# One more batch by seven products, masks loaded into the weights' tiles, and W1's operands split over two stages

## The chip, the cores and the metric

The kernel runs on one core of one Trainium2 chip. The metric is the device time of one launch in microseconds (us). The engines are named PE (matrix products), ACT (ScalarE), DVE (VectorE), POOL (GpSimd) and SP (SyncE). SP, ACT and POOL issue DMA transfers from their own instruction queues.

## The reference

```python
# x: (8, 256, 1024); mask: (8, 1024, 1024) of 0 or 1; W, b, W1, b1: one for all batches
# layer 0
y = x + x @ W.T + b + coeff[:, None, None] * (x @ (2 * mask - 1))
# layer 1: each batch picks one of 32 adapters of rank 16
h = y @ A[adapter]                      # (8, 256, 16)
out = y + y @ W1.T + b1 + 2.0 * (h @ Bm[adapter])
```

Everything is float32. The first layer has another weight matrix in each batch: `I + W.T + coeff * (2 * mask - 1)`. The second layer has one matrix, `I + W1`, for all.

## The kernel before, in words

**Groups.** The eight batches run in two groups of four. For each group comes a first layer, batch by batch, and then a second layer for the four batches together. The output tiles `y` of a group stay on the chip between the two.

**First layer, plain form.** A batch's weight matrix is made in eight pieces of 128x1024 (512 KB). Piece `k` is piece `k % 8` of batch `k // 8`. `load` has SP fetch the mask into an int32 tile `m` of `mpool` (3 tiles), four pieces ahead; it also fetches `x`, `W0` in batch 0, and W1's sixteen blocks `w1` spread over the pieces from 10 on. `build` has ACT turn the mask into `2c*m - c` in a weight tile `w` of `wpool` (3 tiles; L227), and DVE add `W0` (L230), two pieces ahead of the products. `first_batch` (L280) and `first_layer` (L255) multiply; ACT evicts with the bias (L267). Batches 0 to 3 run in this form.

**First layer, seven products.** The class `Seven` splits weights and tokens into 2x2 blocks and needs seven block products in place of eight (L388), at 128 columns each, with the operands `s1` to `s4` (sums of weights, L326) and `t1` to `t4` (sums of tokens, L342). PE's order is X `a11`, Y `a12`, X `s2`, Z `s1`, X `s3`, Z `s4`, X `a22`. X and Z are read in between (L403, L408). Batches 4 to 7 run in this form, with their weights in tiles of `wpool`, `tpool` and `qpool`.

**Second layer.** It takes the seven-product scheme twice, one inside the other: seven outer products `A11, A12, S1, S2, S4, S3, A22`, one call of `run` each, and in each of these seven inner ones with the left operands `a11, s1, s2, a12, s3, a22, s4` ("leaves", 256 KB each, L643). Forty-nine leaves are derived from W1: S1 to S4 are sums of quarters of W1 (`outer`, L539), and each outer operand has its inner sums (`inner`, L522 to L528). `combine_weights` makes them on DVE beside the first layer of group 0, three or four sums after each piece, and `keep` has POOL store each leaf in DRAM (L489). S3 alone is made later, beside runs 1 and 2. `load_leaves` has SP fetch the seven leaves of the next run into `lpool` (7 tiles), as the tiles come free. The right operands are sums of `y`: T1 to T4 (`outer_sum`, L634) and their inner sums `t1` to `t4` (L604 to L610).

Within a run, a bank X gathers four inner products in turn, and each value is read (L694 by ACT where nothing is to be added, L695 by DVE) before the next product adds to it. The next run's first product, `begin`, lies between `s3` and `a22`.

**Adapters.** `begin_adapters` and `load_adapters` clear `lb_pad` and `h_sb` on POOL and issue sixteen small DMAs there: four times `b1` and ones, and for each batch its `la` (64 KB) and rows of `lb_pad`. They hang on a value of `y` of batch 2, half 0. `down` (L675) multiplies `y` by `la` in run 0 of the second layer, after its first two products; `up` (L660) adds the adapters' result through ACT (L669).

**Order.** A scheduler places the instructions on each engine in program order by its own estimate of times, and `tc.issue_after` (in the kernel's words, `behind(...)`) keeps an instruction behind a named one. On the chip each queue runs in that fixed order. Tiles of a pool are given out as they come free.

Of the kernel before, what the change touches and what calls it, by code (L numbers as in the profile page):

```python
# [9 lines left out]
F32 = mybir.dt.float32  # L10
# [9 lines left out]
SEVEN = (4, 5, 6, 7)  # L20
# [4 lines left out]
def kernel(  # L25
# [50 lines left out]
    mpool = ctx.enter_context(tc.tile_pool(name="mask", bufs=3))  # L76
    wpool = ctx.enter_context(tc.tile_pool(name="weff", bufs=3))
# [59 lines left out]
    x_sb, m_sb, weff, raw, weff_at = {}, {}, {}, {}, {}  # L137
# [33 lines left out]
    def load(k: int):  # L171


        b, h, g = pieces[k]
        m_sb[k] = mpool.tile([P, 2, OH], I32, tag="m", name=f"m_{k}")
        pairs = [(m_sb[k], mask[b, g if b == 0 else h * NG + g])]
# [16 lines left out]
        else:  # L193
            for t, a in pairs:
                nc.sync.dma_start(t, a)
# [6 lines left out]
        for n, (q, r) in enumerate(W1_ORDER):  # L202
            if k == 0 and r % 2 == 0:
                two = pair(f"w1_{q}_{r // 2}")
                raw[q, r], raw[q, r + 1] = two[:, 0], two[:, 1]
            if k == 2 * NG + 2 + 3 * n // 4:
                nc.sync.dma_start(raw[q, r], w1T[q, r])

    def build(k: int):
# [8 lines left out]
        if b not in SEVEN or (h == 0 and g < 3):  # L218
            pool, tag = wpool, "w"
        elif g >= NG // 2:  # L220
            pool, tag = tpool, "T"
        else:
            pool, tag = qpool, "q"
        w = pool.tile([P, CG, OH], F32, tag=tag, name=f"w_{k}")
        m = m_sb.pop(k)
# [6 lines left out]
        weff[k] = w  # L232
# [8 lines left out]
    def first_layer(b: int, h: int, y, beside):  # L241
# [3 lines left out]
        for g in range(NG):  # L245
            k = (b * 2 + h) * NG + g
            if k + LOADS_AHEAD < n_pieces:
                load(k + LOADS_AHEAD)
# [22 lines left out]
    def first_batch(y, beside):  # L271

        ps = [bank(f"ps1_0_{i}") for i in range(NC // 2)]
        for c in range(NC):
            load(c + LOADS_AHEAD)
# [26 lines left out]
    H = T // 2  # L302

    class Seven:
# [3 lines left out]
        def __init__(self, b: int):  # L308
            self.b = b
            self.w, self.t = {}, {}  # L310
            self.ps = {}

        def block(self, i, j, a):
# [4 lines left out]
            if k + LOADS_AHEAD < n_pieces:  # L318
                with behind("leaves"):
                    load(k + LOADS_AHEAD)  # L320
# [3 lines left out]
        def weight_sum(self, n, op, x, y, a):  # L324
            s = self.w[n, a] = qpool.tile([P, CG, OH], F32, tag="q", name=f"{n}_{self.b}_{a}")
# [6 lines left out]
        def token_sum(self, n):  # L332
            t = self.t[n] = lpool.tile([P, TPH, H], F32, tag="l", name=f"{n}_{self.b}")
            for a in range(2):
# [7 lines left out]
                nc.vector.tensor_sub(o, x, y)  # L342
# [34 lines left out]
        def half(self, dest, left, right, a, first=False):  # L377
# [4 lines left out]
            for c in range(CG):  # L382
# [4 lines left out]
                for j in range(TPH):  # L387
                    nc.tensor.matmul(  # L388
# [18 lines left out]
        def add(self, i, v, ps):  # L407
            nc.vector.tensor_add(self.out(i, v), ps, self.out(i, v))  # L408

        def products(self):  # L410
# [9 lines left out]
            self.add(0, 0, ps["Y"])  # L420
# [7 lines left out]
            self.with_bias(1, 1, ps["Z"])  # L428
            for a in range(2):
                self.half("X", "s3", "t3", a)  # L430
                yield
            self.add(1, 1, ps["X"])
            for a in range(2):
# [15 lines left out]
    class Sevens:  # L449
# [7 lines left out]
        def begin(self, early: int):  # L457
            while self.made < early:
                next(self.operands, None)
# [31 lines left out]
    later = []  # L491

    def combine_weights():
# [17 lines left out]
        def inner(name, blocks, own, place=None):  # L511
            a11, a12, a21, a22 = (blocks[u, v] for u in range(2) for v in range(2))
            s = {}
            for n in ("s1", "s2", "s3", "s4"):
                if place is None:
                    s[n] = lpool.tile([P, CG, OQ], F32, tag="l", name=f"{name}_{n}")
                else:
                    if n in ("s1", "s3"):
                        two = pair(f"{name}_{n}")
                    s[n] = two[:, n in ("s2", "s4")]  # L520
# [9 lines left out]
                yield  # L530
            for n, t in (("a11", a11), ("a12", a12), ("a22", a22)):
                if n in own:
                    keep(name, n, t)

        def outer(name, op, x, y):
            tiles = [tpool.tile([P, 2, CG, OQ], F32, tag="T", name=f"{name}_{u}") for u in range(2)]
            out = {(u, v): tiles[u][:, v] for u in range(2) for v in range(2)}
# [3 lines left out]
            quads[name] = out  # L541

# [8 lines left out]
        yield from inner("A22", quads["A22"], ("a11", "a22"))  # L551
        yield from outer("S1", nc.vector.tensor_add, quads["A21"], quads["A22"])
        yield from inner("S1", quads["S1"], every)
        yield from outer("S2", nc.vector.tensor_sub, quads["S1"], quads["A11"])
        yield from inner("S2", quads["S2"], every)
# [432 lines left out]
```

## Time and profile before

| | us |
|---|---|
| median of 3 runs | 411.32 |
| lowest and highest | 409.96, 411.5 |
| the profiled execution, its own time | 410.92 |
| its span, from the first to the last instruction | 409.1 |
| PE busy | 403.8 |
| DVE busy | 300.7 |
| first layer of group 0: end of its products | 117.8 |
| second layer of group 0: end of its products | 211.4 |
| first layer of group 1: end of its products | 312.0 |

The profile is of one execution. Its page gives the busy time of each engine, then the span in 40 slices of 10.2 us with the busy share in tenths, the DMA queues, the chain of work that ended last, and the costliest groups of instructions. Timelines list instructions by start time, with the idle time before them and what ended it in brackets. A line such as L255 is a line of the kernel before.

### The profile page before, as it was taken

The page shows a single profiled execution, that of the slowest core. Times are in us where ns is not written, and L with a number is a line of the kernel's source. Part 1 is how long each engine was busy: PE and PEld are TensorE (multiplying, and loading weights), DVE is VectorE, ACT ScalarE, POOL GpSimd, SP SyncE. Part 2 cuts the span into 40 slices and gives each one's busy share as a digit, 9 for nine tenths or more (in the row PEclk, how much of TensorE's full clock was granted, in tenths as well). Part 3 has the DMA queues.
Part 4 walks back from the last instruction along what each step waited for, and adds up shares of the span by engine and source line. Part 5 has one row for each costly group of instructions (what it writes and reads, how often), then busy time and mean ns, then how long its engine had stood idle before and what let it go on. Part 6 is the DMA issues. An engine that isn't in the chain of part 4 may idle for free.

```text
span 409.1 us, 6555 instructions
## 1 busy us (share of the span) xinstructions
PE 403.8 (99%) x2458; PEld 358.2 (88%) x2458; DVE 300.7 (74%) x427; ACT 136.0 (33%) x213; POOL 38.6 (9%) x77
## 2 busy tenths in 40 slices
PE   8999999999999999999999999999999999999996
PEld 6888888888887888888899999999998788888885
DVE  2438598886647558994999999999936365886493
ACT  4434534543445201133115648174221420102200
POOL 0000042575201001000000000400000000000000
PEclk9999999999999999999999999999999999999999
DMA  8999799999987476767795758662122247554654
GB/s 274 405 402 387 274 371 414 412 393 331 414 331 256 134 234 199 220 218 201 241 367 162 263 184 302 202 215 96 26 74 66 75 145 230 173 154 162 213 154 154
DMA packets 41762, 97.44 MB, mean 238 GB/s; under 512 B 5508, under 2 KB 6276, under 8 KB 41732
## 3 DMA queue, kind: packets, MB, share of 16 engines
q1 hardware_dynamic: 32690, 76.17, 55.2%
q0 software_dynamic: 4288, 12.61, 8.1%
q10 hardware_dynamic: 4754, 8.26, 5.4%
q8 instruction: 19, 0.31, 0.3%
q14 instruction: 11, 0.09, 0.1%
HBM read 77.09 MB, written 19.92 MB: 237 GB/s over the span
## 4 chain that ended last, share of the span: by engine, by line
PE 91%; DMA 5%; ACT 2%; SPq 1%; DVE 0%; issue 0%; DVEq 0%; ACTq 0%
PE X L643 24%; PE ps L255 20%; PE X L388 12%; PE Z L643 12%; PE Z L388 6%; PE Y L643 6%; DMA m<-mask 5%; PE ps L280 4%; PE Y L388 3%; PE G L660 2%; PE psh L675 2%; ACT w L227 1%; ACT y L403 0%; SPq L186 0%; DVE w L230 0%
## 5 line engine op out<-in xcount | busy, mean ns | idle before, releaser
L227 ACT ACTIVATE w<-m,neg_c,two_c 128x1024 f32<-128x1024 int32 (+1 forms) x67 | 80.1, 1203 | 109.9 <-DMA m<-mask 40.7
L230 DVE TENSOR_TENSOR w<-w,w_sb 128x1024 f32<-128x1024 f32 (+1 forms) x67 | 77.4, 1172 | 36.9 <-ACT w L227 32.7
L255 PE MATMUL ps<-x,w 128*128 128x256 f32 x384 | 83.3, 379 | 0.0
L255 PEld LDWEIGHTS ps<-x,w 128*128 128x128 f32 x384 | 72.9, 190 | 10.2 <-DVE w L230 0.4
L778 DVE TENSOR_TENSOR c<-c,e 128x512 f32<-128x512 f32 x48 | 32.0, 683 | 3.9 <-ACT c L669 3.8
L388 PE MATMUL X<-t,s 128*128 128x128 f32 x256 | 30.0, 276 | 0.0
L388 PEld LDWEIGHTS X<-t,s 128*128 128x128 f32 x256 | 29.2, 192 | 0.2 <-ACT y L403 0.2
L280 PE MATMUL ps<-x,w 128*128 128x256 f32 x128 | 28.7, 385 | 0.2 <-DVE w L230 0.2
L669 ACT COPY c<-G 128x512 f32<-128x512 f32 x32 | 16.4, 600 | 36.4 <-PE G L660 33.1
L280 PEld LDWEIGHTS ps<-x,w 128*128 128x128 f32 x128 | 24.8, 194 | 4.2 <-DVE w L230 0.8
L695 DVE TENSOR_TENSOR c<-X,c 128x512 f32<-128x512 f32 (+1 forms) x26 | 16.7, 647 | 15.1 <-PE X L643 15.0
L403 ACT ACTIVATE y<-X,b_sb 128x128 f32<-128x128 f32 x48 | 13.6, 366 | 39.6 <-PE X L388 39.6
L694 ACT COPY e<-X 128x512 f32<-128x512 f32 x16 | 9.4, 588 | 48.0 <-PE X L643 41.7
L643 PE MATMUL X<-T_t,l_S_s 128*128 128x256 f32 x96 | 22.8, 380 | 0.0
L643 PEld LDWEIGHTS X<-T_t,l_S_s 128*128 128x128 f32 x96 | 18.2, 190 | 2.7 <-DVE e L695 0.3
L326 DVE TENSOR_TENSOR s<-w,w 128x1024 f32<-128x1024 f32 x16 | 19.2, 1215 | 0.0
L695 DVE TENSOR_TENSOR e<-X,e 128x512 f32<-128x512 f32 x16 | 10.9, 684 | 6.6 <-PE X L643 6.6
L643 PE MATMUL X<-b_t,l_A_s 128*128 128x256 f32 x64 | 15.5, 386 | 0.0
L388 PE MATMUL Z<-x,s 128*128 128x128 f32 x128 | 15.0, 276 | 0.0
L388 PE MATMUL Y<-x,w 128*128 128x128 f32 x128 | 14.9, 275 | 0.0
L388 PE MATMUL Z<-t,s 128*128 128x128 f32 x128 | 14.9, 275 | 0.0
L388 PE MATMUL X<-t,w 128*128 128x128 f32 x128 | 14.9, 275 | 0.0
(125 smaller groups left out, 622.4 us busy)
## 6 DMA issues: line engine op xcount, KB each, us to landing
m<-mask SPq DMA_DIRECT2D x61, 512.0 KB, 6.1
l_S_s<-leaf_S_s SPq DMA_DIRECT2D x32, 256.0 KB, 2.7
x<-xT SPq DMA_DIRECT2D x31, 256.0 KB, 7.8
outT<-c ACTq DMA_DIRECT2D x30, 256.0 KB, 3.5
l_A_s<-leaf_A_s SPq DMA_DIRECT2D x24, 256.0 KB, 2.7
l_S_a<-leaf_S_a SPq DMA_DIRECT2D x24, 256.0 KB, 2.7
w<-w1T SPq DMA_DIRECT2D x16, 256.0 KB, 6.4
leaf_S_s<-S_s POOLq DMA_DIRECT2D x16, 256.0 KB, 7.0
```

The lines of the kernel that those rows point to most:

```text
L227: nc.scalar.activation(w[:, i], m[:, i], AF.Identity, bias=neg_c[:, b : b + 1], scale=two_c[:, b : b + 1])
L230: weff_at[k] = nc.vector.tensor_add(w[:, i], w[:, i], w0_of(k)[:, i])
L255: nc.tensor.matmul(ps[j // 2][:, j % 2, :], lhsT=w[:, c, j * P : (j + 1) * P], rhs=x_sb[b, g][:, c, :],  start=first and j % 2 == 0, stop= ...
L280: nc.tensor.matmul(ps[ot // 2][:, ot % 2, :], lhsT=w[:, h, j * P : (j + 1) * P], rhs=x_sb[0, c // CG][:, c % CG, :], start=c == 0 and ot % ...
L326: anchors["weights"] = op(s, self.w[x, a], self.w[y, a])
L388: nc.tensor.matmul(ps[:, j, :], lhsT=w[:, c, j * P : (j + 1) * P], rhs=r, start=first and a == 0 and c == 0 and j == 0, stop=False, skip_g ...
L403: nc.scalar.activation(self.out(i, v)[:, j, :], ps[:, j, :], AF.Identity, bias=b0_sb[:, ot : ot + 1])
L643: nc.tensor.matmul(ps[:, j, :], lhsT=l[:, c, j * P : (j + 1) * P], rhs=r[:, c, :], start=first and c == 0 and j == 0, stop=False, skip_gro ...
L669: nc.scalar.copy(dest[b // 2][u, b % 2], ps[b])
L694: return nc.scalar.copy(out, ps)
L695: anchors["reads"] = nc.vector.tensor_add(out, ps, other)
L778: nc.vector.tensor_add(o, o, x)
```

## The change

Masks are loaded straight into the weights' tiles, which are seen as int32 until ACT has converted them in place; `mpool` is gone and `wpool` has six tiles. Batch 3 joins the seven-product form. Its weights lie in `tpool` and `wpool`, and its `s3` and `s4` overwrite `a11` and `a12`. W1's blocks are loaded two for each piece from piece 8 on. S2 and S4 are written over A11 and A12, and S1 lies in `qpool`. The inner sums of A22 and S2 are made during batch 3 (`mid`, `late`), those of S4 beside run 0, and S3, whose inputs POOL loads again, beside runs 1 and 2; S4 and S3 are made in place. The adapters are begun in `mid` of batch 3, on a value of its `y`. Masks 32 to 35 are loaded after run 1, and two more after run 5. Group 1's first weights are built beside run 5. The products of the second layer, `up` and `down` are also held in the written order by `behind`.

```diff
-SEVEN = (4, 5, 6, 7)
+SEVEN = (3, 4, 5, 6, 7)
...
-    mpool = ctx.enter_context(tc.tile_pool(name="mask", bufs=3))
-    wpool = ctx.enter_context(tc.tile_pool(name="weff", bufs=3))
+    wpool = ctx.enter_context(tc.tile_pool(name="weff", bufs=6))
...
-        m_sb[k] = mpool.tile([P, 2, OH], I32, tag="m", name=f"m_{k}")
-        pairs = [(m_sb[k], mask[b, g if b == 0 else h * NG + g])]
+        if b in SEVEN and k % (2 * NG) >= 6 and b >= GB:
+            pool, tag = qpool, "q"
+        elif b in SEVEN and b % 2 and k % (2 * NG) < 6:
+            pool, tag = tpool, "T"
+        else:
+            pool, tag = wpool, "w"
+        weff[k] = pool.tile([P, CG, OH], F32, tag=tag, name=f"w_{k}")
+        last = (k + 1) % (GB * 2 * NG) == 0
+        pairs = [(weff[k].bitcast(I32), mask[b, g if b == 0 else h * NG + g])]
...
-            if k == 2 * NG + 2 + 3 * n // 4:
+            if k == 2 * NG + n // 2:
                 nc.sync.dma_start(raw[q, r], w1T[q, r])
...
-        if b not in SEVEN or (h == 0 and g < 3):
-            pool, tag = wpool, "w"
-        elif g >= NG // 2:
-            pool, tag = tpool, "T"
-        else:
-            pool, tag = qpool, "q"
-        w = pool.tile([P, CG, OH], F32, tag=tag, name=f"w_{k}")
-        m = m_sb.pop(k)
+        w = weff[k]
+        m = w.bitcast(I32)
...
+    loaded = 0
+    def load_to(n: int):
+        nonlocal loaded
+        while loaded < min(n, n_pieces):
+            load(loaded)
+            loaded += 1
...
-            if k + LOADS_AHEAD < n_pieces:
-                load(k + LOADS_AHEAD)
+            n = k + LOADS_AHEAD + 1
+            load_to(min(n + max(0, n - (GB - 1) * 2 * NG), GB * 2 * NG))
...
+    SEVEN_AHEAD = 4
+    limit = GB * 2 * NG
...
-            if k + LOADS_AHEAD < n_pieces:
-                with behind("leaves"):
-                    load(k + LOADS_AHEAD)
+            with behind("leaves"):
+                load_to(min(k + SEVEN_AHEAD, max(k + 1, limit)))
             build(k)
...
-            s = self.w[n, a] = qpool.tile([P, CG, OH], F32, tag="q", name=f"{n}_{self.b}_{a}")
+            if self.b < GB and n in ("s3", "s4"):
+                s = self.w[x, a]
+            else:
+                s = qpool.tile([P, CG, OH], F32, tag="q", name=f"{n}_{self.b}_{a}")
+            self.w[n, a] = s
             anchors["weights"] = op(s, self.w[x, a], self.w[y, a])
...
-            self.add(0, 0, ps["Y"])
+            with behind("weights") if self.b < GB else nullcontext():
+                self.add(0, 0, ps["Y"])
...
             self.with_bias(1, 1, ps["Z"])
+            self.mid()
             for a in range(2):
...
             self.add(1, 1, ps["X"])
+            self.late()
             for a in range(2):
...
-        def inner(name, blocks, own, place=None):
+        def inner(name, blocks, own, spare=False):
             a11, a12, a21, a22 = (blocks[u, v] for u in range(2) for v in range(2))
+            for n, t in (("a11", a11), ("a12", a12), ("a22", a22)):
+                if n in own:
+                    keep(name, n, t)
             s = {}
             for n in ("s1", "s2", "s3", "s4"):
-                if place is None:
+                if not spare:
                     s[n] = lpool.tile([P, CG, OQ], F32, tag="l", name=f"{name}_{n}")
...
                     if n in ("s1", "s3"):
-                        two = pair(f"{name}_{n}")
-                    s[n] = two[:, n in ("s2", "s4")]
+                        half = wpool.tile([P, 2, CG, OQ], F32, tag="w", name=f"{name}_{n}")
+                    s[n] = half[:, n in ("s2", "s4")]
                 if n == "s1":
...
                 yield
+        def inner_in_place(name, blocks, own):
+            a11, a12, a21, a22 = (blocks[u, v] for u in range(2) for v in range(2))
             for n, t in (("a11", a11), ("a12", a12), ("a22", a22)):
...
                     keep(name, n, t)
+            yield
+            for n, op, o, x, y in (
+                ("s1", nc.vector.tensor_add, a22, a21, a22),
+                ("s3", nc.vector.tensor_sub, a21, a11, a21),
+                ("s2", nc.vector.tensor_sub, a11, a22, a11),
+                ("s4", nc.vector.tensor_sub, a12, a12, a11),
+            ):
+                op(o, x, y)
+                keep(name, n, o)
+                yield
+        def two(name, pool=qpool, tag="q"):
-        def outer(name, op, x, y):
-            tiles = [tpool.tile([P, 2, CG, OQ], F32, tag="T", name=f"{name}_{u}") for u in range(2)]
-            out = {(u, v): tiles[u][:, v] for u in range(2) for v in range(2)}
+            tiles = [pool.tile([P, 2, CG, OQ], F32, tag=tag, name=f"{name}_{u}") for u in range(2)]
+            return {(u, v): tiles[u][:, v] for u in range(2) for v in range(2)}
...
+        def outer(name, op, x, y, out):
...
+        def again(i, j, out):
+            for (u, v), t in out.items():
+                at = leaf_at.get((f"A{i + 1}{j + 1}", f"a{u + 1}{v + 1}"), w1T[2 * i + u, 2 * j + v])
+                nc.gpsimd.dma_start(t, at)
...
-        yield from inner("A22", quads["A22"], ("a11", "a22"))
-        yield from outer("S1", nc.vector.tensor_add, quads["A21"], quads["A22"])
+        for n, uv in (("a11", (0, 0)), ("a22", (1, 1))):
+            keep("A22", n, quads["A22"][uv])
+        yield from outer("S1", nc.vector.tensor_add, quads["A21"], quads["A22"], two("S1"))
         yield from inner("S1", quads["S1"], every)
-        yield from outer("S2", nc.vector.tensor_sub, quads["S1"], quads["A11"])
-        yield from inner("S2", quads["S2"], every)
-        yield from outer("S4", nc.vector.tensor_sub, quads["A12"], quads["S2"])
-        yield from inner("S4", quads["S4"], every)
-        def rest():
-            yield from outer("S3", nc.vector.tensor_sub, quads["A11"], quads["A21"])
-            yield from inner("S3", quads["S3"], every, pair)
-        later.append(rest())
+        yield from outer("S2", nc.vector.tensor_sub, quads["S1"], quads["A11"], quads["A11"])
+        yield from outer("S4", nc.vector.tensor_sub, quads["A12"], quads["S2"], quads["A12"])
+        def s3():
+            a11, a21 = two("A11"), two("A21", wpool, "w")
+            again(0, 0, a11)
+            again(1, 0, a21)
+            yield
+            yield from outer("S3", nc.vector.tensor_sub, a11, a21, a21)
+            yield from inner_in_place("S3", a21, every)
+        later["A22"] = inner("A22", quads["A22"], (), spare=True)
+        later["S2"] = inner("S2", quads["S2"], every, spare=True)
+        later["S4"] = inner_in_place("S4", quads["S4"], every)
+        later["S3"] = s3()
...
-        def outer_sum(n, x, y, left):
+        def outer_sum(n, x, y, name):
-            big_t[n] = big(f"T{n}", x, y)
-            right[left] = Right(f"T{n}_{group}", big_t[n])
-            yield
-            yield
-            yield from right[left].sums()
-        def inner_sums(left):
-            yield from right[left].sums()
+            big_t[n] = [
+                tpool.tile([P, TPH, T], F32, tag="T", name=f"T{n}_{group}_{v}") for v in range(2)
+            ]
+            right[name] = Right(f"T{n}_{group}", big_t[n])
+            for v in range(2):
+                nc.vector.tensor_sub(big_t[n][v], x[v], y[v])
+                yield
+            yield from right[name].sums()
+        def next_masks(n):
+            with behind("leaves"):
+                if group + 1 < NGROUP:
+                    load_to((group + 1) * GB * 2 * NG + n)
+        def next_weights():
+            for n in range(3 if group + 1 < NGROUP else 0):
+                sevens[group + 1].begin(n + 1)
+                yield
+        def ordered(steps):
+            while True:
+                with behind("reads" if "reads" in own else "layer"):
+                    if next(steps, True):
+                        return
+                yield
...
-        rest = chain(*later) if group == 0 else iter(())
-        load_leaves("A11")
+        own = {}
+        left = {n: ordered(later[n] if group == 0 else iter(())) for n in ("S3", "S4")}
+        with behind("masks"):
+            load_leaves("A11")
         begin(0, "A11", first)
-        for _ in first_steps:
+        for _ in ordered(first_steps):
             pass
+        t1 = ordered(outer_sum(1, b12, b11, "S1"))
...
             0, "A11", first, None, e1,
-            beside=chain(second.sums(), outer_sum(1, b12, b11, "S1")),
+            beside=chain(ordered(second.sums()), islice(left["S3"], 1), islice(t1, 2), left["S4"]),
...
+        t2 = ordered(outer_sum(2, b22, big_t[1], "S2"))
         run(
...
             dest=(0, 0),
-            beside=chain(outer_sum(2, b22, big_t[1], "S2"), islice(rest, 4)),
+            beside=chain(t1, islice(left["S3"], 4), islice(t2, 2)),
...
+        next_masks(4)
...
+            beside=chain(t2, ordered(right["S4"].sums()), left["S3"]),
...
-            beside=outer_sum(3, b22, b12, "S3"),
...
-            beside=outer_sum(4, b21, big_t[2], "A22"),
...
+        nonlocal limit
+        limit = n_pieces
+        run(5, "S3", right["S3"], e1, e1, beside=chain(next_weights(), add_e5()), then=lambda uv: add(c21[uv], e1[uv]))
+        next_masks(6)
...
-        if k == 2 * NG + 3:
+        if k == 2 * NG + 1:
             sums = combine_weights()
         with tc.issue_after(weff_at[min(k + BUILDS_AHEAD, max(weff_at))].ins):
-            for _ in range(3 if k < 4 * NG + 2 else 4):
+            for _ in range(3):
                 next(sums, None)
+        if k >= 5 * NG:
+            sevens[0].begin((1, 2, 4, 6)[k - 5 * NG])
...
-        sevens[group].run(y, between)
...
+        if group == 0:
+            first_batch(y[0], step)
+            for b, h in ((1, 0), (1, 1), (2, 0), (2, 1)):
+                first_layer(b, h, y[b][h], step)
+            for _ in sums:
+                pass
+            def mid(late=y[GB - 1][1][:, 0, H : H + 1]):
+                with behind("weights"):
                     begin_adapters(late)
-                    load_adapters(group, late)
-        for _ in sums:
-            pass
+                    load_adapters(0, late)
+                sums_of("A22")
+                with behind("rows"):
+                    next(later["S4"])
+            def sums_of(name):
+                with behind("weights"), behind("rows"):
+                    for _ in later[name]:
+                        pass
+            sevens[0].batches[-1].mid = mid
+            sevens[0].batches[-1].late = lambda: sums_of("S2")
+        sevens[group].run(y, between)
         anchors["layer"] = anchors["weights"]
-        if group + 1 < NGROUP:
-            sevens[group + 1].begin(3)
         second_layer(group, y, first, first_steps, second)
```

## The prediction

> **What bounds the kernel now.** I read the page's busy rows first, then the chain in order of time, then the timelines of single engines around the places that the change touches. The page:
>
> ```profile
> PE 403.8 (99%) x2458; PEld 358.2 (88%) x2458; DVE 300.7 (74%) x427; ACT 136.0 (33%) x213; POOL 38.6 (9%) x77
> ...
> DMA  8999799999987476767795758662122247554654
> GB/s 274 405 402 387 274 371 414 412 393 331 414 331 256 134 234 199 220 218 201 241 367 162 263 184 302 202 215 96 26 74 66 75 145 230 173 154 162 213 154 154
> ```
>
> PE is never free, so the time is the sum of PE's work plus whatever makes PE wait. The DMA digits show where waits are near: full to 120 us, about half in the second layer of group 0 (118 to 211). From the chain in order of time (start, us, what):
>
> ```profile
> 34.66 83.13 PE ps L255 x384
> ...
> 211.41 3.57 PE X L388 x32
> ```
>
> Three batches in the plain form (L255) take 83.13 us without a gap: 27.71 each, 3.463 for each of its eight pieces. One product of the seven form (L388) takes 3.573, seven take 25.01. The chain's "DMA m<-mask" share around 267 is no lost time: PE's timeline runs through it. So only PE's sum and new PE waits count.
>
> Timelines of ACT and POOL (start, us, instruction), for the waits that I expect:
>
> ```profile
> 47.65 1.70 ACT L267 ACTIVATE y<-ps,b_sb 128x256 f32<-128x256 f32 x4 [1.35 <-PE ps L255]
> 49.24 1.24 ACT L227 ACTIVATE w<-m,neg_c,two_c 128x1024 f32<-128x1024 int32 x1
> ...
> 153.51 0.59 ACT L694 COPY e<-X 128x512 f32<-128x512 f32 x1 [6.32 <-PE X L643]
> ```
> ```profile
> 80.38 0.97 POOL L126 MEMSET lb_pad<- 128x1024 f32 x1
> ...
> 88.00 0.59 POOL L579 DMA_DIRECT2D la<-lora_a  x1 [0.23 <-issue]
> ...
> 91.58 0.58 POOL L579 DMA_DIRECT2D la<-lora_a  x1
> ```
>
> The reader is to see that eviction and conversion share ACT's queue, that a read of a bank costs PE about 0.9 (0.2 to start, 0.59, 0.1 back) unless another product lies between, and that the adapters need 11.2 us on POOL from memset to the issue of the fourth `la`. Landing times by stage (issues of 50 to 80 us, and of 212 to 260):
>
> ```profile
> m<-mask SPq DMA_DIRECT2D x9, 512.0 KB, 9.6
> leaf_A_s<-A_s POOLq DMA_DIRECT2D x12, 256.0 KB, 6.8
> ...
> la<-lora_a POOLq DMA_DIRECT2D x3, 64.0 KB, 3.9
> ```
>
> [...]
>
> **The change part by part** (times of before's profiled execution, 410.92; its span is 409.1 with 1.8 around it).
>
> 1. Batch 3 by seven: PE loses 27.71 and gains 25.01: **-2.7**. VectorE gains 8 weight sums of 1.14 (from the timeline's spacing), 8 token halves of 0.33 and 3 additions of 0.60: +13.6 us. Cover: from 90 to 117 VectorE works 16.5 of 27 us, and the sums of A22, S2 and S4 leave 50 to 100. I followed the changed kernel's instruction order on VectorE with these spacings: `s2` of half 1 is made at about 94.3 and wanted at 99.0, `s4` at 99.0, wanted 108. Zero here, if the DMA keeps up (it costs up to 2 if not).
>
> 2. Masks in the weights' tiles: six tiles wait for PE alone; a mask is issued when piece k-6 is done, 17.3 us ahead of use. A landing of 9.6, ACT's 1.24 and VectorE's 1.22 make 12.1. Zero; the cover of 5.2 gone, each us of later landing is one of PE. Startup loads the same things in the same order: zero, at best -0.5 of the 0.9 that the first three pieces lose.
>
> 3. Order on ACT and VectorE. In the changed order `w_13`'s conversion stands behind batch 1's eviction and its addition behind four sums. Eviction ends at 49.24, sums run from 48.52 to 50.92, the addition to 52.15; PE wants `w_13` at 34.66+5x3.463=51.97: **+0.4** with semaphores (0 to 0.6).
>
> 4. W1 loaded earlier (two per step from piece 8), its sums start right at 49. The eighth `lpool` tile, `A12_s4`, waits for the store of `A11_s1`, issued at 49.9. Landing 6.8 later is 56.7, so `w_15` is ready at 58.5 against 59.2: hidden. With the 9.4 that POOL's stores took at 80 to 110, it is 61.1: 1.9 late. I take **+0.6** (0 to 1.9).
>
> 5. Adapters moved from batch 2 to `mid` of batch 3. POOL starts after product Z (104.4+0.4+0.6=105.4, ACT's first eviction 0.4, copies and start 1.5): first small DMA at 107.2. In before each POOL DMA waited for the landing of the one eight ahead of it (at 84.99 for a store issued at 78.65, at 97.35 for the `la` of 90.40), so `la` begins when the first small one has landed (5.1): 112.2; the fourth is 3.6 later, 115.8, landing after 3.9 to 6.3. PE wants it for `down` at 90.08+25.01+3.46+1.0=119.6. Late by 0.1 to 2.5: **+1.2**. Behind it on PE is all of run 0. POOL's 14 later stores come after `la`, and their leaves are wanted 20 us later: zero.
>
> 6. Masks 32 to 35 (before: 32 to 34 converted at 115 to 122, 35 at 167) are now issued by SP between S1's and S2's leaves, and converted on ACT between the reads of run S1's bank X. Also, the changed PE order puts product `a22` of S1 directly behind `s3`, with no other product between, so PE waits for the read of (1,1): **+1.0** (0.8 to 1.7, if mask 33 also lands late).
>
> 7. The same block of loads is ahead of leaf `S2_a11`. SP issues from the last S1 leaf to `S2_a11`: 2 leaves, 4 masks, 4 x, 3.67 MB; beside them 2 of ACT's c11 stores (0.52) and 3 stores of S3 by POOL (0.79): 4.98 MB. At the 400 to 414 GB/s of the page's fullest slices 12.0 to 12.45 us. The first is issued at 148.32-2.7+2.2 (items 3 to 5)+0.86 (half a product put ahead)=148.7[...]. PE wants it after `a22` and `s4` of S1: 160.2-2.7+2.2+1.0=160.7. **+2.2** (0 without the 1.3 MB of stores, 3.2 at the 377 GB/s of 90 to 117).
>
> 8. S3's inputs are read again by POOL (8 x 256 KB, about 2 MB): issued around 130, wanted at 148: zero; if late, VectorE's T2 and run S2 behind it, up to 1. In-place S4 and S3 need their own leaf stores landed; these have about 5 us: zero.
>
> 9. Of batch 4, weights 32 to 36 are built ahead of run A22's last bank read (before: 32 to 37 and one sum), so VectorE, at 1.14 each, ends `s2` of half 1 at 8.35 after batch 4 begins (before: 7.23); PE wants it at 8.93: **+0.2** (0 to 1.0). Group 1 runs as before: no wait there now, none to gain. The loads that stood behind three mask tiles cost PE nothing.
>
> Sum: -2.7+0.4+0.6+1.2+1.0+2.2+0.2=+2.9, so 413.8 for an execution like the profiled one. The median of the runs shown, 411.32, is 0.40 above it: **414.2**.
>
> **Rivals.** (A, 0.70) The forecast. New waits of 3.4 to 9 us, 412.0 to 417.6; by 0.5% of 411.32, 2.06 us, about what a measurement of this kernel can tell from no change, 0.50 of it is slower and 0.20 the same. For it: PE order and bytes; against: landings are estimates.
> (B, 0.18) Stores do not slow SP's queue. Place: the leaves of S2. SP's 3.67 MB alone need 9.0 us, `S2_a11` lands at 159.7, ahead of 160.7; it decides when the block drains within 10 us. With `la` landing in 3.9 and item 4 hidden, waits are 0.4, 0.1 and 1.0: -1.2, **410.1**; with items 3 and 6 at their low ends, 409.2. Not slower; faster 0.10, same 0.08. For it: leaf loads of 140 to 200 took 3.0 in before's half-full DMA. Against: there SP had no masks beside them.
> (C, 0.12) The DMA engines stay as full as at 90 to 117 (377 GB/s): `A12_s4` 1.9, batch 3's sums 1, adapters 2.5, read 1.7, S2 3.2, turn 0.8, `w_13` 0.4, 11.5 in all. Without batch 3's sums and the turn, which need the worst landing in stages that were emptier before, 9.7-2.7=+7.0: **418.3**. For it: 9.6 for a mask. Against: 414 in other slices.
> That the change does not do what it says is excluded: the changed order has 112 products of 128 columns for batch 3.
>
> **Numbers.** Faster 0.10, same 0.20+0.08, slower 0.50+0.12. The forecast is A's, no mean. Range 409.6 to 418.4: it leaves out the lower half of B and the upper half of C, 0.15.
>
> **What would show it.** PE rows of batch 3 on L408 with 3.57 a product; PE gaps at about 52, 120, 156 and 161, named `w`, `la`, `e` and `l_S_a`; no mask wait in batches 5 to 7. The second layer of group 0, 211.41-117.79=93.6 in before, would be 98.0 (items 5 to 7). Item 4 shows as a VectorE wait for the store of an A12 tile near 56; item 5 as POOL's `la` issues near 112 to 116. The forecast is wrong if that layer is no longer than before, or if PE waits for masks before 50 us or in batch 3, which I cost at nothing.

## The result, and the profile after

The changed kernel takes **416.73 us** (median of 6, 416.02 to 417.72), the kernel before 411.02. The ratio is 1.0142 [1.0125, 1.0159]: slower by 5.7 us. The profiled execution of the changed kernel took 416.53, its span is 414.4 against 409.1. Ratios leave out executions that took over 1.5% more than the fastest of the same kernel, which of all runs here are two of `spread`, 422.61 and 423.12. A line such as L695 is from here on a line of the changed kernel; in a kernel of an experiment the same line can stand up to seven lines lower.

The page of the kernel after: PE's row, the granted clock and the DMA rows.

```profile
PE 403.4 (97%) x2554; PEld 358.7 (87%) x2554; DVE 312.0 (75%) x446; ACT 137.5 (33%) x221; POOL 42.8 (10%) x85
...
PEclk9999999999999998999999999999999999999999
DMA  8999999960389999766699857732113247655654
GB/s 289 405 402 395 402 412 418 408 269 2 98 294 365 320 315 405 242 195 226 209 358 396 317 160 251 272 121 58 27 52 74 80 127 236 171 154 158 220 156 152
```

PE's busy time hardly falls (403.8 to 403.4) though batch 3 needs less work; one slice of the clock is below full. The DMA engines, nearly full to 117 before, are now empty from 93 to 104 and a third busy from there to 114 (2 and 98 GB/s), and busy after. What PE waited for, in total us, times and longest:

```profile
PE X L695 <- ACT e L749: 3.8, 2, 3.2
...
PE X L408 <- ACT y L423: 1.1, 1, 1.1
...
PE ps L267 <- DVE w L234: 0.3, 1, 0.3
```

PE's timeline (start, us, what; in brackets the idle time before and its end), in five places: batch 1, batch 3, `down`, run S1 and the turn, where group 0's second layer ends and group 1 begins.

```profile
34.46 17.43 PE L267 MATMUL ps<-x,w 128*128 128x256 f32 x80
52.17 38.25 PE L267 MATMUL ps<-x,w 128*128 128x256 f32 x176 [0.28 <-DVE w L234]
90.26 3.73 PE L408 MATMUL X<-x,w 128*128 128x128 f32 x32
...
111.70 3.74 PE L408 MATMUL X<-t,w 128*128 128x128 f32 x32
115.27 1.89 PE L695 MATMUL X<-y,l_A_a 128*128 128x256 f32 x8
117.00 1.89 PE L695 MATMUL Z<-b_t,l_A_s 128*128 128x256 f32 x8
118.82 3.65 PE L730 MATMUL psh<-y,la 128*16 128x256 f32 x64
...
151.32 1.89 PE L695 MATMUL Y<-T,l_S_a 128*128 128x256 f32 x8
156.38 3.50 PE L695 MATMUL X<-T_t,l_S_s 128*128 128x256 f32 x8 [3.16 <-ACT e L749]
160.55 1.99 PE L695 MATMUL X<-T_t,l_S_a 128*128 128x256 f32 x8 [0.68 <-ACT e L749]
162.38 1.89 PE L695 MATMUL Z<-T,l_S_s 128*128 128x256 f32 x8
164.37 1.97 PE L695 MATMUL X<-T,l_S_a 128*128 128x256 f32 x8
...
219.25 3.74 PE L408 MATMUL Y<-x,w 128*128 128x128 f32 x32
224.13 2.05 PE L408 MATMUL X<-t,s 128*128 128x128 f32 x16 [1.14 <-ACT y L423]
```

I count PE's **excess**: from the start of one product to the start of the next, less what it takes with nothing in its way (1.73 for eight matmuls of 256 columns, 3.57 for 32 of 128). After 25 us it is 10.9 here and 3.0 in the kernel before. The 7.9 more are 0.45 at `w_13` (before 52), 3.33 ahead of run S1's product `s3` and 2.44 from its start to that of `a22` (156.38 to 160.55), 1.31 at the turn, and 0.4 in bits. Less the 2.7 of batch 3 that is 5.2, and the spans differ by 5.3. From the second layer's first product to batch 4's Y it is 103.98 (115.27 to 219.25), in the kernel before 97.19 (117.63 to 214.82).

The 2.44 has two parts: 0.7 of it is a wait; the rest is that the eight matmuls take 3.50 and not 1.89. The windows view of the kernel after (window, length, busy us of PE, PEld, DVE, ACT and POOL with counts, granted clock, DMA share, GB/s) says why:

```profile
153.10:156.30 3.20, 0.11 (x1) 0.00 (x0) 3.20 (x6) 1.69 (x2) 0.00 (x0) 0.96 0.98 364
156.30:159.80 3.50, 3.42 (x8) 2.50 (x8) 0.40 (x1) 1.26 (x2) 0.00 (x0) 0.55 1.03 415
```

After the gap of 3.16 us PE's granted clock is 0.55 for 3.5 us; from 160 to 164 it is 1.00 again.

What held the read is on ACT's timeline, and why on SP's:

```profile
144.65 5.34 ACTq L754 DMA_DIRECT2D outT<-c  x4
154.61 1.24 ACT L231 ACTIVATE w<-w,neg_c,two_c 128x1024 f32<-128x1024 int32 x1 [9.46 <-DMA outT<-c]
155.76 0.56 ACT L749 COPY e<-X 128x512 f32<-128x512 f32 x1
```
```profile
147.69 0.33 SPq L203 DMA_DIRECT2D w<-mask  x1
148.06 0.49 SPq L207 DMA_DIRECT2D x<-xT  x1
...
154.76 0.33 SPq L203 DMA_DIRECT2D w<-mask  x1
155.13 0.46 SPq L207 DMA_DIRECT2D x<-xT  x1
155.71 0.40 SPq L685 DMA_DIRECT2D l_S_a<-leaf_S_a  x1
```

Mask 32 leaves SP at 147.69 and lands 6.8 later, at 154.5. Its conversion, at 154.61, stands on ACT ahead of the read of (0,1), which PE's `s3` needs and which could have been made near 151.5. (The trace names an `outT` store that landed at the same moment; in `spread` below the same wait, 8.99 to 154.31, is named `w<-mask`.) Leaf `S2_a11`, at the end of the block, leaves at 155.71 and takes 8.5: 164.2. PE begins with it at 164.37, with no wait on record.

### The profile page after: what moved, and what is told of

It is laid out like the page before. It is cut to its first block, busy times and chain, and to the rows that moved or that the text cites. A ratio compares the mean times of both kernels' runs of the same rounds, so it can differ in the third digit from the quotient of the medians.

```text
span 414.4 us, 6761 instructions
## 1 busy us (share of the span) xinstructions
PE 403.4 (97%) x2554; PEld 358.7 (87%) x2554; DVE 312.0 (75%) x446; ACT 137.5 (33%) x221; POOL 42.8 (10%) x85
## 4 chain that ended last, share of the span: by engine, by line
PE 90%; DMA 4%; DVE 2%; ACT 1%; issue 1%; SPq 1%; DVEq 0%; ACTq 0%
PE X L695 24%; PE X L408 17%; PE ps L267 12%; PE Z L695 11%; PE Z L408 9%; PE Y L695 5%; PE ps L292 4%; PE Y L408 3%; PE G L713 2%; PE psh L730 2%; DMA outT<-c 2%; DMA w_sb<-w0T 2%; DMA w<-mask 1%; DVE w L234 1%; SPq L194 1%
## 5 line engine op out<-in xcount | busy, mean ns | idle before, releaser
L231 ACT ACTIVATE w<-w,neg_c,two_c 128x1024 f32<-128x1024 int32 (+1 forms) x67 | 79.9, 1203 | 72.6 <-DMA w<-mask 45.8
L267 PE MATMUL ps<-x,w 128*128 128x256 f32 x256 | 55.7, 379 | 0.3 <-DVE w L234 0.3
L267 PEld LDWEIGHTS ps<-x,w 128*128 128x128 f32 x256 | 48.6, 190 | 7.2 <-DVE w L234 0.7
L408 PE MATMUL X<-t,s 128*128 128x128 f32 x288 | 33.9, 275 | 1.1 <-ACT y L423 1.1
L292 PE MATMUL ps<-x,w 128*128 128x256 f32 x128 | 28.2, 381 | 0.5 <-DVE w L234 0.5
L292 PEld LDWEIGHTS ps<-x,w 128*128 128x128 f32 x128 | 24.3, 191 | 4.6 <-DVE w L234 1.2
L695 PE MATMUL X<-T_t,l_S_s 128*128 128x256 f32 x96 | 24.4, 399 | 3.2 <-ACT e L749 3.2
L750 DVE TENSOR_TENSOR e<-Y,e 128x512 f32<-128x512 f32 x8 | 5.5, 689 | 27.5 <-PE Y L695 15.7
L695 PEld LDWEIGHTS X<-T_t,l_S_s 128*128 128x128 f32 x96 | 19.1, 201 | 6.8 <-ACT e L749 3.6
L408 PE MATMUL X<-t,w 128*128 128x128 f32 x192 | 22.4, 275 | 0.0
L408 PEld LDWEIGHTS X<-t,w 128*128 128x128 f32 x192 | 21.9, 192 | 0.0
L408 PE MATMUL X<-x,w 128*128 128x128 f32 x160 | 19.0, 275 | 0.0
L408 PEld LDWEIGHTS X<-x,w 128*128 128x128 f32 x160 | 18.7, 192 | 0.2
L408 PE MATMUL Z<-t,s 128*128 128x128 f32 x160 | 18.8, 275 | 0.0
```

Source lines behind the costliest of these rows:

```text
L231: nc.scalar.activation(w[:, i], m[:, i], AF.Identity, bias=neg_c[:, b : b + 1], scale=two_c[:, b : b + 1])
L267: nc.tensor.matmul(ps[j // 2][:, j % 2, :], lhsT=w[:, c, j * P : (j + 1) * P], rhs=x_sb[b, g][:, c, :],  start=first and j % 2 == 0, stop= ...
L292: nc.tensor.matmul(ps[ot // 2][:, ot % 2, :], lhsT=w[:, h, j * P : (j + 1) * P], rhs=x_sb[0, c // CG][:, c % CG, :], start=c == 0 and ot % ...
L408: anchors["products"] = nc.tensor.matmul(ps[:, j, :], lhsT=w[:, c, j * P : (j + 1) * P], rhs=r, start=first and a == 0 and c == 0 and j == ...
L695: anchors["inner"] = nc.tensor.matmul(ps[:, j, :], lhsT=l[:, c, j * P : (j + 1) * P], rhs=r[:, c, :], start=first and c == 0 and j == 0, s ...
L750: own["reads"] = anchors["reads"] = nc.vector.tensor_add(out, ps, other)
```

## The experiments

All times are ratios to the kernel before on the same chip, with a 95% interval where both were timed repeatedly. Each edit is made to the changed kernel; comments in the excerpts of code say where a line stands or in which version.

**1 to 3. Two waits, one over the other?** `hold` puts the conversions of batch 4 behind ACT's last read, and changes ACT's order alone. `spread` loads one mask after each of four runs. `spread_hold` does both.

```diff
-            nc.scalar.activation(w[:, i], m[:, i], ...)
+            with behind("copies") if k // (2 * NG) == GB else nullcontext():
+                nc.scalar.activation(w[:, i], m[:, i], ...)
...
-                return nc.scalar.copy(out, ps)
+                anchors["copies"] = nc.scalar.copy(out, ps)
+                return anchors["copies"]
```
```diff
-        next_masks(4)
+        next_masks(1)
...
+        next_masks(2)   # ahead of run(3, "S2", ...)
+        next_masks(3)   # ahead of run(4, "S4", ...)
+        next_masks(4)   # ahead of run(5, "S3", ...)
```

> The changed kernel with only ACT's order altered: the conversions of masks 32 to 35 stand behind the three reads of run S1's bank X that ACT makes, not between them. SP's queue stays as it is. In the changed kernel run S1 from Y (151.32) to the first product of run S2 (164.37) holds 5.3 us more than its four products and one bare read. Theory 1, two waits lie over each other there: leaf a11 of S2 is issued by SP at 155.7, behind masks and x, and lands 8.5 later at 164.2, whatever ACT does. The reads come early, the gap moves to the first product of S2 and is named l_S_a; gain 0 to 0.6, time 416.2 to 416.7. Theory 2, only ACT's queue costs: the leaf is in time and 5.3 us are gained, 411.4.

Measured: 1.0182 [1.0165, 1.0199], 419.04, which is 2.3 over theory 1's range. PE's timeline of this kernel:

```profile
154.59 1.89 PE L696 MATMUL X<-T_t,l_S_s 128*128 128x256 f32 x8
157.16 1.99 PE L696 MATMUL X<-T_t,l_S_a 128*128 128x256 f32 x8 [0.68 <-ACT e L750]
158.99 1.90 PE L696 MATMUL Z<-T,l_S_s 128*128 128x256 f32 x8
165.05 3.75 PE L696 MATMUL X<-T,l_S_a 128*128 128x256 f32 x8 [4.16 <-DMA l_S_a<-leaf_S_a]
```

Theory 1's mechanism holds: `s3` follows Y at once, and the gap stands at the leaf (issued at 156.53, landing 8.4 later). No gain is left: the gap is longer and the products behind it are slower by 3.0 (clock 0.50 from 165 to 170). (0.9 more is lost at 142, at leaf `S1_a11`, ahead of the edit.) The 0.84 between `s3` and `a22` is the bare read of item 6.

> Masks 32 to 35 with their x are loaded one after each of the runs A12, S1, S2 and S4, not all four after A12; ACT's first conversion (mask 32) still stands ahead of the read of (0,1). Theory 1: the leaves of S2 are in time; what stays of the 5.3 us is the read behind mask 32, which was issued at 147.7 and lands 5 to 7 later: 1.5 to 3.3. The planner puts a product back between s3 and a22, 0.9 more. Gain 2.5 to 4.5, time 412.2 to 414.2. Theory 2 (ACT's queue alone, mainly mask 32): gain 1 to 3, 413.7 to 415.7. Theory 3 (only the leaf): gain 5 to 6, 410.7 to 411.7.

Measured: 1.0114 [1.0094, 1.0135], near 415.9, by 1.7 outside theory 1's range. (Theory 2's range ends 0.2 below it, but `hold` has ruled that theory out.) The ratio rests on two executions, 415.81 and 416.15; the traced one took 419.93. In its trace run S1 does what theory 1 says: product `a11` of S2 needs no leaf wait, and 3.5 stay behind mask 32 (2.19 of gap, 1.34 of slow products at a clock of 0.60). But run S3 has a new gap, 3.45 of excess, and 1.74 after it.

> Both: masks 32 to 35 one after each run, and their conversions behind run S1's reads. Theory 1: both waits are gone, 5.3 to 6.2 us gained, 410.5 to 411.4. Theory 2 (the ACT queue alone): as with the conversions held alone, near 411.4. Theory 3 (bandwidth of the DMA engines in this stage, whatever the order of the bytes): less than 3 us gained, over 413.7.

Measured: 1.0151 [1.0107, 1.0196], near 417, 6 over theory 1's number and where theory 3 put it (over 413.7). But theory 3's place is wrong: run S1 has only a short wait left (PE's timeline), as theory 1 says, and a gap is now in run S3, 40 us on. Its cause is on VectorE's timeline:

```profile
153.16 1.89 PE L696 MATMUL X<-T_t,l_S_s 128*128 128x256 f32 x8
155.63 1.97 PE L696 MATMUL X<-T,l_S_a 128*128 128x256 f32 x8 [0.58 <-DVE T_t L665]
...
191.99 1.89 PE L696 MATMUL Y<-T,l_S_a 128*128 128x256 f32 x8
197.15 2.95 PE L696 MATMUL X<-T_t,l_S_s 128*128 128x256 f32 x8 [3.27 <-DVE e L752]
```
```profile
195.27 1.23 DVE L235 TENSOR_TENSOR w<-w,w_sb 128x1024 f32<-128x1024 f32 x1 [2.71 <-ACT w L232]
196.41 0.68 DVE L752 TENSOR_TENSOR e<-X,e 128x512 f32<-128x512 f32 x1
```

An addition of a weight waits 2.71 for its conversion, which ACT starts at 194.00 after 2.69 of idle time that a DMA ends (the mask's, in the author's reading), and run S3's read stands behind it: the mechanism of run S1, on another engine. That both waits of S1 are there is shown by the three runs together; that their removal gains time is not, until `best2w` below.

**4 and 5. The turn.** `turn` puts the conversions of batch 5 behind batch 4's first eviction; `turn_q` also gives the last half store to POOL.

```diff
+            with behind("evicted") if b == GB + 1 else nullcontext():
                 nc.scalar.activation(w[:, i], m[:, i], ...)
...
-    store(out[1, 0][:, c], *dest, 1, 0, c, (nc.sync, nc.scalar)[c])
+    store(out[1, 0][:, c], *dest, 1, 0, c, (nc.sync, nc.scalar if group else nc.gpsimd)[c])
```

> The changed kernel with the turn to group 1 altered alone: ACT evicts batch 4's bank X ahead of the conversions of w_40 and w_41, and the last half of group 0's output is stored by POOL's queue, not by ACT's. In the changed kernel this eviction starts at 222.94 though product X ended near 219.3, and the PE loses 1.1 to 1.3 us to it. Theory: ACT's queue, with conversions to 221.65 and a store at 222.55 that waits, holds the eviction; gain 1.1, time 415.6, PE's gap at 224 gone. Rival: VectorE's s2 of half 1, ready near 222.7 at the 1.14 spacing, is as late; gain 0.1 or less, the gap stays and is named s.

> As the run of the turn before it, but the last store stays in ACT's queue: only the conversions of w_40 and w_41 go behind batch 4's first eviction. If the conversions held the eviction, the gap at the turn is 0 as in the first version, if the store's wait (for an older store to land) held it, the eviction starts at the same place, near 222.9 of the changed kernel's count, and the excess of 1.3 us stays.

Measured: `turn_q` 1.0143 [1.0093, 1.0193], `turn` 416.1 in one execution. ACT's and PE's timelines of `turn`:

```profile
219.75 1.14 ACT L424 ACTIVATE y<-X,b_sb 128x128 f32<-128x128 f32 x4 [7.36 <-DMA outT<-c]
220.76 4.64 ACT L232 ACTIVATE w<-w,neg_c,two_c 128x1024 f32<-128x1024 int32 x4
```
```profile
219.34 3.74 PE L409 MATMUL Y<-x,w 128*128 128x128 f32 x32
222.92 1.95 PE L409 MATMUL X<-t,s 128*128 128x128 f32 x16
```

The gap of 1.31 is gone in both, so the conversions held the eviction, not VectorE, and not the store, which in `turn` still stands ahead of it. Half comes back 8 us later (0.68 and 0.64), at the next eviction behind conversions. Gains of this size can't be told in the times.

**6 to 8. Other places for the masks, and the backlog.** `shift_all` loads each mask one run earlier than `spread`; `pool_all` has POOL load them (`queue = nc.gpsimd` for the four pieces). Both hold the conversions and alter the turn. `early_ad` begins the adapters on batch 2, half 0, so that POOL is free for the leaf stores:

```diff
                 first_layer(b, h, y[b][h], step)
+                if (b, h) == (2, 0):
+                    late = y[2][0][:, 0, :1]
+                    begin_adapters(late)
+                    load_adapters(0, late)
```

> Masks 32 to 35 one by one, one run earlier than in the spread version (ahead of runs A12, S1, S2 and S4), all conversions behind run S1's reads, and the turn as altered before. Theory: every wait named so far is gone. Of the spread and held version's 10.5 us of PE excess after 115, the 5.2 of run S3 (a read behind w_35's addition on VectorE) and 0.7 of the turn go; 4.5 stay, against 1.7 in the kernel before and 2.4 won in batch 3: 411.6 (411.0 to 412.2). Rival: each mask in front of a run's leaves makes that run's first leaf late, one gap of 2 us or more comes back in run S1, S2, S4 or S3: 413.5 or more.

> Masks 32 to 35 and their x are loaded by POOL's queue, not SP's: x ahead of the adapters, where the DMA engines are nearly idle, the masks behind the stores of S2's leaves near 128. SP has leaves alone in runs A11 to S4. Conversions held and the turn altered as in the other. Theory (what hurts is the order in SP's and ACT's queues): as good as the shifted version, 411.0 to 412.2. Rival (what hurts is the bytes that share the DMA engines, on whatever queue): leaves of S1 are late by 1 to 3 us near 140, 413 to 415.

> The changed kernel with the adapters begun again on a value of batch 2 (POOL is idle from 69 to 106 there), so that the stores of the fourteen leaves of A22 and S2, 3.7 MB, leave POOL when VectorE has made them (104 to 111.5) and not behind the adapters (115.9 to 124.9). The DMA engines are nearly idle from 92 to 115 and full from 120 to 164 in the changed kernel. Theory 1 (the block of masks itself makes S2's leaf late; the stage before 147 matters little): product a11 of S2 still starts at 163 to 164.4, time 415.6 to 416.7. Theory 2 (the backlog of late stores and of what stands behind them is the cause): leaf S2 a11 and mask 32 land 3 to 5 us earlier, time 411.5 to 414.

Measured: `shift_all` 1.0166 [1.0142, 1.019], `pool_all` 1.0118 [1.0101, 1.0135], `early_ad` 1.0133 [1.0117, 1.0148]. PE's timelines of the first and of the last:

```profile
138.80 1.89 PE L699 MATMUL Y<-y,l_A_a 128*128 128x256 f32 x8
143.68 1.97 PE L699 MATMUL X<-T,l_S_a 128*128 128x256 f32 x8 [2.99 <-DMA l_S_a<-leaf_S_a]
```
```profile
154.75 1.99 PE L695 MATMUL X<-T_t,l_S_s 128*128 128x256 f32 x8 [1.67 <-ACT e L749]
158.28 1.99 PE L695 MATMUL X<-T_t,l_S_a 128*128 128x256 f32 x8 [1.53 <-ACT e L749]
160.11 1.89 PE L695 MATMUL Z<-T,l_S_s 128*128 128x256 f32 x8
164.59 1.96 PE L695 MATMUL X<-T,l_S_a 128*128 128x256 f32 x8 [2.60 <-DMA l_S_a<-leaf_S_a]
```

In `shift_all` the rival is right (its gap in run S1, and a time over 413.5): one mask ahead of run S1's leaves makes the first of them land 8.0 after its issue, and PE waits 3.0. In `pool_all` PE waits 2.7 in the same place with the masks on another queue, at 398 GB/s, and its time, 415.47, is 0.5 above the rival's range. That would fit the engines' bytes and not only the order in SP's queue. But the trace names VectorE there and has no landing for that leaf, so the cause stays open. `early_ad` moves the stores (340 GB/s against 75 from 108 to 112), mask 32 comes earlier (the first gap is 1.67, not 3.16), and yet `S2_a11` starts at 164.59, and the time, 416.41, is theory 1's. The reads' waits shrink, the leaf's grows, and their sum stays (6.4 of excess in this stage, 6.0 in the changed kernel), which is `hold` once more from the other side.

**9 to 12. Each wait in its turn.** `best2` joins `early_ad`, the held conversions and the turn, with two masks ahead of run A11 and two ahead of A12. `best2w` also puts `w_36`'s addition behind run S3's reads. `best3` moves a third mask ahead of A11 and the fourth behind A12, converts `w_13` ahead of batch 1's eviction, and makes run S4's read ahead of T4. `best4` is `best3` with the masks as in `best2w`.

```diff
         with behind("masks"):
             load_leaves("A11")
+        next_masks(2)   # best3: 3
...
+        next_masks(4)   # ahead of run(1, "A12", ...); best3: ahead of run(2, "S1", ...)
...
+            with behind("S3 read") if k == GB * 2 * NG + 4 else nullcontext():   # best2w on
                 weff_at[k] = nc.vector.tensor_add(w[:, i], w[:, i], w0_of(k)[:, i])
...
+            with behind("converted") if (b, h) == (1, 0) else nullcontext():   # best3, best4
                 nc.scalar.activation(y[:, j, :], ...)
```

> All together: adapters on batch 2, two masks with x ahead of run A11 and two ahead of run A12 (their tiles are free once those stores have landed), conversions behind run S1's reads, the turn as altered before. Theory: the gap of 3.15 us at run S1 that the shifted version had goes, since 3.7 MB of stores and the masks lie ahead of that stage; what stays of PE's excess is 0.45 in batch 1, 0.85 and 1.0 in runs S4 and S3 and the 3.0 that the kernel before has too; with 2.7 won in batch 3 the time is near the kernel before: 411.0 (410.3 to 411.8). Rival: masks ahead of A12's leaves make them late in the same way as before, a gap of 2 us or more with half the clock after it: 413 to 415.

> As the combined version, and w_36's addition on VectorE, which waits for mask 36 ahead of run S3's reads, stands behind them. Theory: the 1.0 of run S3 goes as well, 410.0 (409.5 to 411.0). Rival: the addition is missed at the turn, where VectorE is full, and the 1 us comes back there: as the combined version.

> The version before it had PE's time back to the old kernel's, with three waits of 0.45 (w_13 behind batch 1's eviction on ACT), 0.76 (leaf S1 a11 behind two masks) and 0.85 us (run S4's read of (0,1) behind a sum T4 on VectorE) left. Here w_13 is converted ahead of that eviction, three masks go ahead of run A11 and the fourth after run A12, and run S4's read stands ahead of T4. Theory: each wait was put down to its real cause and no other lies under it; 2.1 us less, 408.9 (408.3 to 409.6), ratio to the kernel before 0.994 to 0.997. Rival: one more layer, the wait under each is as long as the one above it (a third mask makes A12's leaves late, the fourth S2's): 410.5 to 412.

> The placement of masks goes back to two ahead of run A11 and two ahead of run A12. Of the version before it only the two orders stay: w_13 converted ahead of batch 1's eviction (0.45) and run S4's read ahead of T4 (0.85). Both were gone from PE's waits in that version. Theory: 1.3 us less than the 410.9 measured with this placement of masks, 409.6 (409.0 to 410.3), ratio to the kernel before 0.995 to 0.999. Rival: the waits were hiding others of the same length in runs S4 and S3, as the gap of S1 did: 410.5 to 411.2, no difference from the kernel before.

| kernel | ratio | PE's excess after 25 us, and its largest parts |
|---|---|---|
| before | 1 | 3.0: none over 0.4 |
| after | 1.0142 | 10.9: S1 5.8, turn 1.3, `w_13` 0.45 |
| `best2` | 1.0064 [1.0041, 1.0086] | 7.3: turn 1.2, S3 1.1, S4 0.85, S1 leaf 0.8 |
| `best2w` | 1.0008 [0.9995, 1.002] | 5.1: S4 0.85, S1 leaf 0.8, `w_13` 0.45 |
| `best3` | 1.0139 [1.0102, 1.0176] | 12.3: A12's leaf 6.7, S2's leaf 2.2, S4 0.75 |
| `best4` | 1.0001 [0.9987, 1.0015] | 4.8: S4 0.75, A12's leaf 0.6, S1 0.5 |

`best2`, at 412.91, is 1.1 over its theory's range: the turn's next eviction (1.2) and S1's leaf (0.8) were not counted. The rival, A12's leaves late by 2 or more, is not seen in it. `best2w`, at 410.93, in its theory's range, is 2.3 us better by the ratios: the 1.1 of run S3 is gone and, in its new order at the turn, the 1.2 there. Of the changed kernel's excess it is rid of run S1's 5.8 and the turn's 1.3, with 1.6 of new waits (S4 and S1's leaf). By the ratios it takes 5.5 us less, and its excess is 5.8 less, so the waits at run S1 and at the turn account for the slowdown. In `best3`, at 417.39, the rival's place is right (PE's timeline), a third mask ahead of A12's leaves, but a gap of 3.29 and the clock after it (0.50 from 132.1 to 135.6, 0.60 to 138.6) put the time 5.4 over the rival's 412.

```profile
132.09 3.78 PE L701 MATMUL X<-y,l_A_a 128*128 128x256 f32 x8 [3.29 <-DMA l_A_a<-w1T]
135.66 3.06 PE L701 MATMUL X<-b_t,l_A_a 128*128 128x256 f32 x8
```

`best4`: the waits at `w_13` and at run S4's read of (0,1) are gone, and others stand in their place, one of them at S4's next read (what PE waited for in it):

```profile
PE X L701 <- DVE c L757: 0.6, 1, 0.6
...
PE X L701 <- DVE T_t L670: 0.4, 1, 0.4
PE X L701 <- DMA l_A_a<-w1T: 0.4, 1, 0.4
```

So its rival, no difference in time, is right as well, though two of the three waits stand in runs A12 and S1 and not in S4 and S3. No version beats the kernel before; the two that match it still carry 1.8 to 2.1 of excess more than it does, which takes most of batch 3's 2.7.

## Why the prediction was right or wrong

Slower was right, the range held the time, and the forecast of 414.2 was 2.5 too low; rival C's 418.3 is 1.6 too high. The second layer of group 0 was to grow by 4.4 and grew by 6.8. That the sum came as near as it did is in part luck: 4.0 of the 5.6 us of waits in it (items 4, 5 and 7) don't show, and most of what does show, at run S1 and at the turn, was not in it. By its steps:

- **Item 1**, batch 3: right. Its products start at 90.26 and end at 115.27, 25.01, with no gap.
- **Items 2 and 8**, zero: right. PE's one wait for a weight tile before 50 is 0.55 at 17.09 (0.17 at 17.13 in the kernel before), and PE is no later by it, 34.46 against 34.50 at batch 1's first product. No wait stands in batch 3, and none names a re-read of S3's inputs.
- **Item 3**, +0.4: right, 0.45, named `w` and at 52, as foretold.
- **Item 4**, +0.6: too large, 0. VectorE's `A12_s4` starts at 56.37 after a wait of 0.2; `w_15` is added from 56.98.
- **Item 5**, +1.2: too large, 0. POOL issued the four `la` about where it was foretold:

```profile
111.27 0.59 POOL L639 DMA_DIRECT2D la<-lora_a  x1
...
114.84 0.58 POOL L639 DMA_DIRECT2D la<-lora_a  x1
```

  but the last landed 2.0 after its issue, at 116.8, and `down` starts at 118.82, as long after the product ahead of it (1.82) as in the kernel before. The step took landing times from full DMA engines, and here they moved 2 and 98 GB/s in the two slices before. It looked at the stage before the change, which the change itself empties.
- **Item 6**, +1.0: the term that was mis-sized, 5.8 in the trace. The bare read was priced well (0.84 in `hold`, 0.9 foretold). The step let only mask 33 be late. Mask 32, issued at 147.69 and landing 6.8 later, was the late one: it stood ahead of the read that PE wanted at 151.5. And the step priced waits as idle time alone, where the gap of 3.16 was followed by 3.5 us at a clock of 0.55, another 1.7. A lower clock was left out of every estimate. Whether the 1.7 cost time here is not shown: four of the six executions had a mean clock of 1.000 and took 416.02 to 416.94, the two at 0.996 took 416.53 and 417.72. The late leaf of item 7 would have held PE in any case.
- **Item 7**, +2.2: its mechanism is right, its size is not, and the way it was added failed. The leaf landed at 164.2, not 162.9. PE, undelayed by items 4 and 5, would have wanted it near 159.1 (Y at 151.32, `s3` at 153.05, a read of 0.84, then `a22` and `s4`), not at 160.7. It was 5.1 late, and none of it shows, since item 6's gap covers it. The sum put the two in a row; they lie over each other, and the longer counts. `hold` shows it by taking the upper one away, `early_ad` by shrinking it. The 162.9 was the author's estimate: the first issue at 148.7, 12.25 for the bytes, and a fixed part. That part can be estimated from the kernel before: the median landing of its leaf loads, 2.7, less 0.6 for 256 KB at 414 GB/s, is 2.1.
- **Item 9**, +0.2: wrong cause, 1.31. VectorE's two sums were in time; the step left out ACT's queue at the turn, where the conversions of `w_40` and `w_41` stood ahead of the eviction.

Rival B falls with the leaf's 164.2 (it needed 159.7). Rival C's price of full engines fits the block of masks better than item 7's: from 147.2 to 164.2 the engines moved 364 GB/s at a busy share of 0.99 (C took 377, which puts the leaf at 163.9; item 7 took 400 to 414, reached only from 156 on, 403 to 416). But its waits at items 4, 5 and in batch 3 are not there, so its number is near for a reason that is only in part its own. The places named in "What would show it" were right at 52 and 156; at 120 and 161 there is next to nothing, and the turn was missed.

## What to carry to other kernels

When a prefetch is moved into a busy stage, follow it on three queues: what stands behind its transfer in the issuing queue, what stands behind its first use on each engine (on ACT the read at 155.76, on VectorE the one at 196.41 in `spread_hold`), and when the consumer really wants that; the later of them sets the cost, not their sum. A wait that is found and removed is worth only what lies between it and the next one: test that by taking the upper one away alone, before the gain is counted. Keep an instruction that waits for a far transfer (a conversion, its addition) behind the reads of the product in progress, on every engine.

## What was not expected of the hardware

- A gap in PE's work can be followed by slow products and so by more loss than its length. In the traces here every gap of over 3 us between products was: 3.16 by 1.7 us of loss (clock 0.55), 3.29 in `best3` by 3.1 and 4.16 in `hold` by 3.0 (clock 0.50 in both). But 2.04 in `spread` was enough for 1.3 of loss (clock 0.60), while 2.60 in `early_ad` and 2.99 in `shift_all` cost nothing more (clock 1.00 in both), nor did 2.07 in `best3` (the product behind it took 1.97). So it isn't the length alone that decides.
- The same kernel can then have two times. `shift_all` took 414.57 and 415.49 at a mean clock of 0.999 and 1.000, and 417.72 to 418.79 at 0.995 to 0.996; `spread` 415.81 and 416.15 at 1.000, and 419.93 at 0.992, and the trace of this last has 3.5 of slow products. That the clock fell behind the same gaps in some executions and not in others would explain both, but it is not shown: of each kernel only one execution was traced. The changed kernel has no such difference (416.02 to 416.94 at 1.000, 416.53 and 417.72 at 0.996): its slow products lie in a stretch in which PE would have waited for a leaf anyway.
- A leaf of 256 KB landed 8.0 to 8.5 us after its issue where the DMA engines moved 390 to 416 GB/s; the medians over the whole run of the changed kernel are 2.7 to 2.9. So the price of a late load was set here by the stage in which it was issued.
